# Two graph layers in one kernel: when the second layer's weights are loaded and combined, and the order of the last quad

## The chip, the cores and the metric

The kernel runs on one core of a Trainium2 chip. The metric is the device time of one execution in microseconds (us), lower is better. TensorE is called PE here, VectorE DVE, ScalarE ACT, GpSimd POOL and SyncE SP. SP computes nothing; it issues most of the DMA transfers, in order. POOL issues others between its computations.

## The reference

There are 128 graphs of 128 nodes with 512 features, all in fp32. In short:

```
h  = relu(layernorm(x))
# layer 0: attention over the graph, three hops
Xw = h @ Wv0 + bv;  sj = Xw @ aw[:512];  si = Xw @ aw[512:]
e  = leaky_relu(sj[:, None, :] + si[:, :, None] + ab, 0.2)
A  = adj * exp(e);  T = A / (sum(A, -1) + 1e-12)
x1 = x + relu(sum over k = 0, 1, 2 of (T^k h) @ Wk[k] + bk[k])
# layer 1
h2 = relu(layernorm(x1))
q, k = split(h2 @ Wqk);  v = h2 @ Wv1
w  = (512 ** -0.5) * mask * rowsum(q * (adj @ (k * mask)))
out = x1 + softmax(w over the nodes)[:, :, None] * v
```

The kernel folds q and k of layer 1 into one 512x512 matrix `M = Wq Wk^T`, so that w needs `h2 M` and `adj h2` alone. Layer 1 therefore multiplies h2 by one 512x1024 matrix, `rl`: its first half is M, its second `Wv1`.

## The kernel before

**Products.** Every large product is done with seven block products in place of eight (`strassen`, and `one_round` in layer 1): the blocks of the right matrix are combined by four subtractions (`combine`), those of the left by four more (`left_sums`, `inner_sums`), and the sums of the products are formed partly in the PSUM banks a, b, c and e. There are two sets of banks, `set1` (a1, b1, c1, e1) and `set2`. The chain inside a round is always the same: product 1 into a, ACT copies a to b; product 5 into e, ACT copies e to s; product 6 into b, ACT copies b to c; product 2 into a, which ends block (0, 0); product 7 into c, ACT copies c to s, and e + s ends block (1, 1); product 3 into b, b + s ends (0, 1); product 4 into c ends (1, 0).

**Layer 0** goes over 64 pairs of graphs (`for p in range(NP)`). PE multiplies by `r10` (`y10`, the hops 1 and 0), applies the transition matrix of the pair (`inner`, `outer`), and multiplies the pair after the next by `r2` (`y2`). Between these stand, on DVE, the block-wise transposes of h (`x<-hv`, L340) and their sums, the layer norm statistics, the attention, the transpose of the transition matrix (`tt<-junk`), and the sum that gives x1 (L616). A transpose takes a round trip through DRAM: h goes out (`hd<-h`, or `h2d<-h` for layer 1), comes back by blocks in four loads (`hv<-hd`, `hv<-h2d`), and DVE transposes 32x32 blocks. The transition matrix goes the same way (`td<-t`, `junk<-td`). For layer 1 the transposed h2 of a pair and its four sums are collected in `fw` (`for_layer1`, L407 to 441, one pair later) and stored as `fd` when a quad of graphs is complete, in two halves.

**The weights of layer 1.** `rl` is 512x1024. Its first half is computed in the setup, its second is loaded there (`rows(rl[:, :, 1], wv1)`). One outer combine (four subtractions of 128x1024) in pair 2 gives seven factors of 512x512 (`FACTORS`). In pairs 3 to 9 `prepare` combines one factor each (four subtractions of 128x256, into `stage`) and stores it to DRAM as `rwd`: one store of 512 KB and three of 128 KB. In pair 10 four of the seven factors are loaded as `rw`, the other three at the start of layer 1.

**Order.** A scheduler places the instructions of each engine; `behind(what, op)` tells it to issue an instruction only after the one recorded as `done[what]`. Since every engine and every DMA queue works in order, these marks fix who stands in front of whom. In layer 1 the order is written by hand: `put` (L651) chains each engine's instructions, and so do `dve`, `act`, `pool`, `sync` and `swdge`, as well as `ordered` for PE.

**Layer 1** goes over 32 quads (two pairs). Outer factors 1, 5, 2, 6 and then 3, 7, 4 are worked off in rounds, each of seven inner products of 128x256 a factor. `together` runs two rounds side by side, one step of each in turn; a dictionary of hooks says what other work follows each step. Outer results are added in `c`, a tile of four parts (`c[:, 0:4]`). Two of them, when complete, are `h2 M` of the two pairs and are multiplied with `agg = adj h2` for the scores (`scores`); the other two are the values. The scores of a quad lie in columns; to take the softmax over the nodes they are spread over rows, by a transpose and a round trip through DRAM (`spread_scores`, `pwd`, `pw`), and then DVE finds the peak (`peaks`), ACT takes exponentials (`exp_own`, `exp`), DVE the factor (`factors`), ACT scales the values (`scale`), POOL adds x1 by a DMA that accumulates (`add_x1`), and SP stores (`store`). All this runs one to two quads behind the products. The last quad (q = 31) has its own code: rounds (1, 6) and (2, 7) side by side, then 4, 5 and 3 by steps, and its two pairs of scores are spread by transposes on PE (`spread_pair`).

Of the kernel before, what the change touches and what calls it, by code (L numbers as in the profile page):

```python
# [16 lines left out]
def kernel(  # L17
# [32 lines left out]
    G = 2  # L50
# [136 lines left out]

    def combine(r, t):


        nc.vector.tensor_sub(t[0], r[0, 1], r[0, 0])
        nc.vector.tensor_sub(t[1], r[1, 1], t[0])
        nc.vector.tensor_sub(t[2], r[1, 1], r[0, 1])
        done["right"] = nc.vector.tensor_sub(t[3], r[1, 0], t[1]).ins
        return dict(zip((5, 6, 7, 4, 1, 2, 3), t + [r[0, 0], r[1, 0], r[1, 1]]))
# [81 lines left out]
    def statistics(src, gate="warm", middle=None):  # L277
# [13 lines left out]
        behind("aT" if middle else "warm", nc.vector.tensor_mul, r[:, 2], r[:, 1], r[:, 1])  # L291
# [34 lines left out]
    def by_blocks(h, hd=None):  # L326

        hd = dram.tile([G, P, D], FP, name="hd") if hd is None else hd
        nc.sync.dma_start(hd.rearrange("g n d -> n g d"), h)
        hv = front.tile([P, G, Q, P], FP, name="hv")  # L330
        v = hd.rearrange("g (q b) (c i) -> c b (g q) i", b=S32, i=P)
        for c in range(DC):
            at = hv[c * S32:(c + 1) * S32].rearrange("p g q i -> p (g q) i")
            done["hv"] = nc.sync.dma_start(at, v[c]).ins  # L334
        return hv
# [27 lines left out]
    def strassen(banks, left, right, s, first, ends, steps={}, gate="warm", seventh="warm"):  # L363
# [16 lines left out]
        done["ba"] = behind("warm" if first or "h2" not in done else "h2", nc.scalar.copy, b, a).ins  # L380
# [24 lines left out]
    SUMS = {}  # L405

    def for_layer1(p):  # L407
# [13 lines left out]
        if second:  # L421
# [3 lines left out]
            queue = nc.gpsimd if q + 1 < NQ else nc.sync  # L425

            def store_half(i):
                half = slice(4 * i, 4 * i + 4)
                queue.dma_start(fd[:, half].rearrange("p o n -> p (o n)"), fv[:, half].rearrange("p o n -> p (o n)"))  # L429

            def upper():
                behind("c12", nc.vector.tensor_sub, at[7], at[1], fv[:, L21])
                done["c12"] = nc.vector.tensor_sub(at[3], at[2], at[6]).ins
                store_half(1)
# [144 lines left out]
    def y10(p, steps):  # L579
# [6 lines left out]
        def end11(e, t):  # L586
# [8 lines left out]
            (1, 0): lambda c: None}, steps, "warm" if p else "z")  # L595
# [24 lines left out]
    def norm2(p):  # L620
# [6 lines left out]
        HV2[p] = by_blocks(h, H2D[p])  # L627
# [9 lines left out]

    def prepare(o, stage):
# [3 lines left out]
        combine(r, [t[:, i] for i in range(4)])  # L642
        behind("x1d", nc.sync.dma_start, RWD[o][:, :4], t)
        for i, at in enumerate(((0, 0), (1, 0), (1, 1))):
            behind("x1d", nc.sync.dma_start, RWD[o][:, 4 + i], r[at])
# [78 lines left out]
    with tc.issue_after(done["hv"]):  # L724
        load_x(3)
        load_adj(2)
        rows(rl[:, :, 1], wv1)
# [3 lines left out]
    for p in range(NP):  # L731
        def between():
# [6 lines left out]
            if p + 3 < NP:  # L739
                RS0[p + 3] = behind("left", statistics, xg[p + 3])  # L740
            if p == 2:
                rightl.update(behind("rs", combine, {(kh, k): rl[:, kh * HC:(kh + 1) * HC, k]
                                                     for kh in range(2) for k in range(2)},
                                     [tl[:, i] for i in range(4)]))
            if 3 <= p < 3 + len(FACTORS):
                behind("rs", prepare, FACTORS[p - 3], stage)
# [13 lines left out]
        if p > 0:  # L760
            behind("c12", for_layer1, p - 1)
        if p == NP - 2:
# [11 lines left out]
        behind("c12" if p else "left", outer, p, z)  # L774
        if p + 4 < NP:
            load_x(p + 4)
        if p == 0:
# [23 lines left out]
        if p == 3 + len(FACTORS):  # L801
# [3 lines left out]
            RW = {}  # L805
            for o in FACTORS[:4]:
                RW[o] = early.tile([P, 7, HD], FP, name=f"rw{o}")
                nc.sync.dma_start(RW[o], RWD[o])
# [34 lines left out]
    load_left(1, sync, (0,))  # L843
    load_left(1, swdge, (1,))
# [4 lines left out]
    def one_round(q, banks, factors, s, ends):  # L849
# [17 lines left out]
        def p5():  # L867
            product(e, 5, True)
            copy(s[:, 0], e)
# [9 lines left out]
        def p7():  # L879
            product(c, 7)  # L880
            copy(s[:, 1], c)
            ends[1, 1](v[3], sv[:, 1])

        def p3():
            product(b, 3)
            ends[0, 1](v[1], sv[:, 0])
# [111 lines left out]
    def catch_up(q):  # L998
# [4 lines left out]
        PW[q - 1] = spread_scores(W[q - 1])  # L1003
# [24 lines left out]
    for q in range(NQ - 1):  # L1028
# [28 lines left out]
        hooks = {0: sums[:2], 1: sums[2:]}  # L1057
        if q > 0:
# [23 lines left out]
    catch_up(q)  # L1082
    c, (s1, s2) = C[q], S.pop(q)
    x1 = back[2].tile([P, 2, G, D], FP, name="h2")
    for i in range(2):
        sync(x1[:, i], X1D[2 * q + i].rearrange("g n d -> n g d"))
    last_block(prior)
    soft = {}


    together(one_round(q, set1, (1, 6), s1, plain_ends(lambda i, j: c[:, 0:2, i, j])),
             one_round(q, set2, (2, 7), s2, adding_ends(
                 lambda i, j: c[:, 2:4, i, j],
                 lambda i, j: c[:, 0:1, i, j].to_broadcast([P, 2, HD]), True)),
             {2: lambda: scale(late, 1, 0), 3: lambda: scale(late, 1, 1)})
    add_x1(late, 1)

    dve(nc.vector.tensor_add, outer(q, 3), outer(q, 3), outer(q, 1))
    dve(nc.vector.tensor_add, outer(q, 1), outer(q, 0), outer(q, 1))
    soft[2] = peaks(W[prior], PW.pop(prior))  # L1100
    aggregate(q)
    for pair in range(2):
        store(late, pair)
    scores(q, 0, c[:, 2])


    r4 = one_round(q, set1, (4,), s1, adding_ends(lambda i, j: c[:, 0:1, i, j],
                                                  lambda i, j: c[:, 3:4, i, j], True))

    def sum_of_p5(end):  # L1110

        def both(*args, at):
            end(*args)
            for to in (1, 3):
# [103 lines left out]
```

## Time and profile before

| what | value |
|---|---|
| time, median of 3 runs | 2251.65 us (2249.95 to 2254.73) |
| the profiled execution's own time | 2251.06 us |
| its span, first to last instruction | 2249.3 us |
| PE busy | 2212.1 us, 98% |
| DVE, ACT, POOL busy | 74%, 55%, 31% |
| mean granted clock of PE | 0.996 |
| chain that ended last | PE 85%, DMA 6%, DVE 5% |
| DMA | 523.82 MB, 233 GB/s over the span |

Layer 0 lasts until about 1440 us, layer 1 from there to the end; the last quad starts at 2209. "Busy" counts from the first to the last element of an instruction. A granted clock of 1.00 is full speed, and 0.50 half of it.

### The profile page before, as it was taken

The page shows a single profiled execution, that of the slowest core. Times are in us where ns is not written, and L with a number is a line of the kernel's source. Part 1 is how long each engine was busy: PE and PEld are TensorE (multiplying, and loading weights), DVE is VectorE, ACT ScalarE, POOL GpSimd, SP SyncE. Part 2 cuts the span into 40 slices and gives each one's busy share as a digit, 9 for nine tenths or more (in the row PEclk, how much of TensorE's full clock was granted, in tenths as well). Part 3 has the DMA queues.
Part 4 walks back from the last instruction along what each step waited for, and adds up shares of the span by engine and source line. Part 5 has one row for each costly group of instructions (what it writes and reads, how often), then busy time and mean ns, then how long its engine had stood idle before and what let it go on. Part 6 is the DMA issues. An engine that isn't in the chain of part 4 may idle for free.

```text
span 2249.3 us, 29447 instructions
## 1 busy us (share of the span) xinstructions
PE 2212.1 (98%) x8109; PEld 1537.4 (68%) x8109; DVE 1666.1 (74%) x4524; ACT 1240.8 (55%) x2870; POOL 700.6 (31%) x828
## 2 busy tenths in 40 slices
PE   9999999999999999999999999999999999999997
PEld 5665656666566666666666666578888888888886
DVE  5777768777777777877778777577767767776777
ACT  3554545555554555545555555456666666666665
POOL 2121112121121211212112111145555555555554
PEclk9999999999999999999999999999999999999999
DMA  7688998777787887888778786767788888888887
GB/s 193 182 258 255 263 275 246 229 230 235 225 245 218 240 240 219 242 228 229 240 225 235 229 230 202 262 220 230 223 245 233 243 224 250 225 231 243 236 243 193
DMA packets 426467, 523.82 MB, mean 233 GB/s; under 512 B 100522, under 2 KB 281386, under 8 KB 409918
## 3 DMA queue, kind: packets, MB, share of 16 engines
q1 hardware_dynamic: 384876, 397.36, 58.7%
q0 software_dynamic: 41136, 124.04, 21.3%
q8 instruction: 65, 1.06, 0.2%
q14 instruction: 100, 0.82, 0.1%
q10 hardware_dynamic: 290, 0.53, 0.1%
HBM read 297.62 MB, written 224.18 MB: 232 GB/s over the span
## 4 chain that ended last, share of the span: by engine, by line
PE 85%; DMA 6%; DVE 5%; SPq 1%; ACT 1%; issue 1%; POOL 0%; DVEq 0%; ACTq 0%; POOLq 0%
PE a L91 25%; PE b L91 22%; PE c L91 22%; PE e L91 15%; DMA td<-t 1%; DMA hv<-h2d 1%; DMA hv<-hd 1%; SPq L334 1%; DMA tl<-in_L_gnn_Wqk_dram 1%; DMA pw<-pwd 1%; DMA atd<-aT 1%; DMA pwd<-pwt 1%; SPq L530 0%; DMA h2d<-h 0%; DVE fw L419 0%
## 5 line engine op out<-in xcount | busy, mean ns | idle before, releaser
L655 POOL TENSOR_TENSOR c<-s,c 128x512 f32<-128x512 f32 (+1 forms) x186 | 200.1, 1090 | 258.5 <-DVE s L655 253.7
L111 POOL DMA_DIRECT2D agb<-in_adj_dram x256 | 149.7, 591 | 340.9 <-DVE aT L86 248.2
L91 PE MATMUL a<-r,x 128*128 128x512 f32 x512 | 240.8, 592 | 0.2 <-issue 0.2
L91 PE MATMUL b<-rw,in 128*128 128x256 f32 x896 | 215.8, 381 | 0.1
L91 PEld LDWEIGHTS b<-rw,in 128*128 128x128 f32 x896 | 170.9, 191 | 23.9 <-ACT b L655 0.5
L429 POOL DMA_DIRECT2D fd<-fw x62 | 34.7, 559 | 477.4 <-DVE fw L437 283.6
L91 PEld LDWEIGHTS a<-r,x 128*128 128x128 f32 x512 | 97.1, 190 | 96.3 <-issue 92.9
L86 ACT COPY s<-c 128x257 f32<-128x257 f32 (+1 forms) x128 | 61.4, 479 | 174.6 <-PE c L91 174.5
L655 POOL TENSOR_TENSOR c<-c 128x1024 f32<-128x1024 f32 (+1 forms) x70 | 152.1, 2182 | 13.3 <-DVE c L655 13.0
L86 ACT COPY b<-a 128x257 f32<-128x257 f32 (+1 forms) x128 | 59.4, 464 | 165.8 <-PE a L91 165.8
L86 DVE TENSOR_TENSOR e<-e,s 128x512 f32<-128x512 f32 x64 | 44.7, 698 | 141.8 <-ACT s L86 141.8
L91 PE MATMUL a<-w,x 128*128 128x257 f32 x512 | 131.9, 380 | 1.2 <-DVE x L340 1.2
L91 PE MATMUL b<-w,sx 128*128 128x257 f32 x512 | 132.0, 380 | 0.0
L91 PE MATMUL b<-t,sx 128*128 128x512 f32 x256 | 120.6, 593 | 4.0 <-ACT b L86 4.0
L655 DVE SCALAR_TENSOR_TENSOR junk<-agg,wscale,c 128x512 f32<-128x512 f32 x128 | 98.7, 771 | 30.7 <-POOL c L655 25.8
L91 PE MATMUL c<-t,x 128*128 128x512 f32 x256 | 120.5, 593 | 0.2 <-ACT s L86 0.2
L91 PE MATMUL c<-t,sx 128*128 128x512 f32 x256 | 120.4, 593 | 0.0
L91 PE MATMUL e<-t,sx 128*128 128x512 f32 x256 | 120.3, 592 | 0.0
L91 PE MATMUL b<-r,sx 128*128 128x512 f32 x256 | 120.3, 592 | 0.0
L655 ACT ACTIVATE c<-c,wcol 128x512 f32<-128x512 f32 x125 | 87.1, 719 | 59.2 <-DVE wcol L655 58.3
L91 PE MATMUL c<-rw,in 128*128 128x256 f32 x448 | 109.0, 383 | 2.8 <-ACT c L655 2.7
L419 DVE STREAM_TRANSPOSE fw<-hv 128x256 f32<-128x256 f32 x256 | 90.9, 413 | 26.9 <-DMA hv<-h2d 26.8
(253 smaller groups left out, 5250.0 us busy)
## 6 DMA issues: line engine op xcount, KB each, us to landing
fd<-fw POOLq DMA_DIRECT2D x62, 1024.0 KB, 5.1
x1d<-x SPq DMA_DIRECT2D x64, 512.0 KB, 5.8
h2d<-h SPq DMA_DIRECT2D x64, 512.0 KB, 3.2
hv<-h2d SPq DMA_DIRECT2D x256, 128.0 KB, 4.2
xg<-in_x_dram SPq DMA_DIRECT2D x63, 512.0 KB, 6.1
hd<-h SPq DMA_DIRECT2D x63, 512.0 KB, 3.1
hv<-hd SPq DMA_DIRECT2D x252, 128.0 KB, 4.0
f<-fd SPq DMA_DIRECT2D x31, 1024.0 KB, 6.3
```

Source lines behind the costliest of these rows:

```text
L86: return op(*args, **how)
L91: done["mm"] = op(*args, **how).ins
L111: nc.gpsimd.dma_start(agb[p][c * S32:(c + 1) * S32].rearrange("p g q i -> p (g q) i"), v[c])
L334: done["hv"] = nc.sync.dma_start(at, v[c]).ins
L419: done["c12"] = nc.vector.transpose(blocks[:, k, j].rearrange("p f (n b) -> p f n b", n=Q), hv[:, j].rearrange("p n (k f a) -> p k f n a", ...
L429: queue.dma_start(fd[:, half].rearrange("p o n -> p (o n)"), fv[:, half].rearrange("p o n -> p (o n)"))
L655: done[engine] = op(*args, **how).ins
```

## The change

It has five parts.

1. Layer 1's weights are handled in single pieces over 19 pairs. Pairs 1 to 4 load one quarter of Wv1 each. Pairs 5 to 8 do one subtraction of the outer combine each, behind the transposes of `fw` and in front of x1. Pairs 9 to 15 prepare one factor each: two subtractions stand inside `statistics`, between ACT's logarithm and what DVE makes of it, the other two where the outer subtractions stood. Its four stores follow x1d on SP. Pairs 16 to 19 load one `rw` each.
2. In the last pair of layer 0 the copy b<-a no longer waits for the relu of h2 (`second`). The second half of `fd` 30 is stored by SP, between `h2d<-h` and `hv<-h2d` of the last pair, in place of POOL, and both halves of the left side of quad 1 are loaded by POOL.
3. In quad 0 the left sums for quad 1 follow steps 3 and 4 of the second group of rounds, no longer steps 0 and 1. In quad 1 the exponentials start one step later.
4. In the last quad, round (2, 7) lags round (1, 6). Banks are added where they lie with fewer copies (`direct`, `early`), further sums go to POOL (`u2`, `on_p5`). The scores of the quad before it are spread by four transposes on PE in place of the round trip through DRAM.
5. The rounds 4, 5 and 3 of the last quad change sets of banks and order; the scaled finish by ACT and POOL (`finish_scaled`) is dropped for a fourth `finish` on DVE.

The order of PE's instructions is the same up to the last quad.

```diff
+    def combine_steps(r, t):
+        def step(i, a, b):
+            done["right"] = nc.vector.tensor_sub(t[i], a, b).ins
+        return [partial(step, 0, r[0, 1], r[0, 0]), partial(step, 1, r[1, 1], t[0]),
+                partial(step, 2, r[1, 1], r[0, 1]), partial(step, 3, r[1, 0], t[1])]
+    def combined(r, t):
+        return dict(zip((5, 6, 7, 4, 1, 2, 3), t + [r[0, 0], r[1, 0], r[1, 1]]))
-        nc.vector.tensor_sub(t[0], r[0, 1], r[0, 0])
-        nc.vector.tensor_sub(t[1], r[1, 1], t[0])
-        nc.vector.tensor_sub(t[2], r[1, 1], r[0, 1])
-        done["right"] = nc.vector.tensor_sub(t[3], r[1, 0], t[1]).ins
-        return dict(zip((5, 6, 7, 4, 1, 2, 3), t + [r[0, 0], r[1, 0], r[1, 1]]))
+        for step in combine_steps(r, t):
+            step()
+        return combined(r, t)
...
-    def statistics(src, gate="warm", middle=None):
+    def statistics(src, gate="warm", middle=None, last="aT"):
...
-        behind("aT" if middle else "warm", nc.vector.tensor_mul, r[:, 2], r[:, 1], r[:, 1])
+        behind(last if middle else "warm", nc.vector.tensor_mul, r[:, 2], r[:, 1], r[:, 1])
...
-    def by_blocks(h, hd=None):
+    def by_blocks(h, hd=None, between=None):
+        if between:
+            between()
...
-    def strassen(banks, left, right, s, first, ends, steps={}, gate="warm", seventh="warm"):
+    def strassen(banks, left, right, s, first, ends, steps={}, gate="warm", second="warm", seventh="warm"):
...
-        done["ba"] = behind("warm" if first or "h2" not in done else "h2", nc.scalar.copy, b, a).ins
+        done["ba"] = behind(second, nc.scalar.copy, b, a).ins
...
-    SUMS = {}
+    SUMS, LAST = {}, []
...
-            queue = nc.gpsimd if q + 1 < NQ else nc.sync
+                queue = nc.gpsimd if q + 1 + i < NQ else nc.sync
-                store_half(1)
+                if q == NQ - 2:
+                    LAST.append(partial(store_half, 1))
+                else:
+                    store_half(1)
...
-            (1, 0): lambda c: None}, steps, "warm" if p else "z")
+            (1, 0): lambda c: None}, steps, "warm" if p else "z",
+            second="h2" if 0 < p < NP - 1 else "warm")
...
-        HV2[p] = by_blocks(h, H2D[p])
+        HV2[p] = by_blocks(h, H2D[p], LAST.pop() if p == NP - 1 else None)
...
+    FIRST = 1 + 2 * DC
+    OUTER = ({(kh, k): rl[:, kh * HC:(kh + 1) * HC, k] for kh in range(2) for k in range(2)}, [tl[:, i] for i in range(4)])
-        combine(r, [t[:, i] for i in range(4)])
-        behind("x1d", nc.sync.dma_start, RWD[o][:, :4], t)
-        for i, at in enumerate(((0, 0), (1, 0), (1, 1))):
-            behind("x1d", nc.sync.dma_start, RWD[o][:, 4 + i], r[at])
+        def store_all():
+            behind("x1d", nc.sync.dma_start, RWD[o][:, :4], t)
+            for i, at in enumerate(((0, 0), (1, 0), (1, 1))):
+                behind("x1d", nc.sync.dma_start, RWD[o][:, 4 + i], r[at])
+        return combine_steps(r, [t[:, i] for i in range(4)]), store_all
...
-        rows(rl[:, :, 1], wv1)
+        weights, weights_end = [], None
+        if DC < p <= 2 * DC:
+            weights = combine_steps(*OUTER)[p - DC - 1:p - DC]
+            weights_end = lambda: rightl.update(combined(*OUTER))
+        elif FIRST <= p < FIRST + len(FACTORS):
+            weights, weights_end = prepare(FACTORS[p - FIRST], stage)
...
-                RS0[p + 3] = behind("left", statistics, xg[p + 3])
-            if p == 2:
-                rightl.update(behind("rs", combine, {(kh, k): rl[:, kh * HC:(kh + 1) * HC, k]
-                                                     for kh in range(2) for k in range(2)},
-                                     [tl[:, i] for i in range(4)]))
-            if 3 <= p < 3 + len(FACTORS):
-                behind("rs", prepare, FACTORS[p - 3], stage)
+                two = weights[:2] if len(weights) > 2 else []
+                RS0[p + 3] = behind("left", statistics, xg[p + 3],
+                                    middle=(lambda: [behind("aggr", step) for step in two]) if two else None, last="right")
...
+        for step in weights[-2:]:
+            behind("c12", step)
+            done["c12"] = done["right"]
...
+        if weights:
+            weights_end()
+        if 0 < p <= DC:
+            behind("x1d", rows, rl[:, :, 1], wv1, (p - 1,))
...
-        if p == 3 + len(FACTORS):
+        if p == FIRST + len(FACTORS):
-            RW = {}
-            for o in FACTORS[:4]:
-                RW[o] = early.tile([P, 7, HD], FP, name=f"rw{o}")
-                nc.sync.dma_start(RW[o], RWD[o])
+            RW = {o: early.tile([P, 7, HD], FP, name=f"rw{o}") for o in FACTORS[:4]}
+        if FIRST + len(FACTORS) <= p < FIRST + len(FACTORS) + 4:
+            o = FACTORS[p - FIRST - len(FACTORS)]
+            behind("x1d", nc.sync.dma_start, RW[o], RWD[o])
...
-    load_left(1, sync, (0,))
-    load_left(1, swdge, (1,))
+    load_left(1, swdge)
-    def one_round(q, banks, factors, s, ends):
+    def one_round(q, banks, factors, s, ends, direct=False, early=None):
...
-            copy(s[:, 0], e)
+            if early:
+                early(v[3])
+            else:
+                copy(s[:, 0], e)
...
-            copy(s[:, 1], c)
-            ends[1, 1](v[3], sv[:, 1])
+            if early:
+                ends[1, 1](v[2])
+            elif direct:
+                ends[1, 1](v[2], sv[:, 0])
+            else:
+                copy(s[:, 1], c)
+                ends[1, 1](v[3], sv[:, 1])
-            ends[0, 1](v[1], sv[:, 0])
+            if early:
+                ends[0, 1](v[1])
+            else:
+                ends[0, 1](v[1], sv[:, 0])
...
-    def catch_up(q):
+    def catch_up(q, spread=True):
-        PW[q - 1] = spread_scores(W[q - 1])
+        if spread:
+            PW[q - 1] = spread_scores(W[q - 1])
...
-        hooks = {0: sums[:2], 1: sums[2:]}
-        if q > 0:
+        hooks = {3: sums[:2], 4: sums[2:]}
+        if q == 1:
+            hooks = {0: sums[:2],
+                     1: [lambda: exp_own(*soft), lambda: exp(*soft, 0)] + sums[2:],
+                     2: [lambda: exp(*soft, 1)],
+                     3: [lambda: exp(*soft, 2), lambda: exp(*soft, 3)],
+                     4: [lambda: factors(*soft)],
+                     5: [lambda: scale(prior, 0, 0)],
+                     6: [lambda: scale(prior, 0, 1)]}
+        elif q > 0:
...
-    catch_up(q)
...
+    catch_up(q, False)
+    c, (s1, s2) = C[q], S.pop(q)
...
+    def c_(k, i, j):
+        return c[:, k, i, j]
+    def in_place(to):
+        return lambda bank: dve(nc.vector.tensor_add, to, bank, to)
+    def u2(i, j):
+        pool(nc.gpsimd.tensor_add, c_(1, i, j), c_(0, i, j), c_(1, i, j))
+    def on_p5(i):
+        pool(nc.gpsimd.tensor_add, c[:, 2:4, i, 1], c[:, 0:2, i, 1], s2[:, 0].rearrange("p (k d) -> p k d", k=2))
+    def from_u2(i, j):
+        return lambda bank: dve(nc.vector.tensor_add, c[:, 2:4, i, j], bank, c[:, 0:2, i, j])
+    def on_top(i, j):
+        return lambda bank, t: in_place(c[:, 2:4, i, j])(bank)
+    ra = one_round(q, set1, (1, 6), s1, plain_ends(lambda i, j: c[:, 0:2, i, j]), direct=True)
+    rb = one_round(q, set2, (2, 7), s2, {(0, 0): from_u2(0, 0), (1, 1): on_top(1, 1), (0, 1): on_top(0, 1),
+                                         (1, 0): from_u2(1, 0)}, direct=True)
+    def a_h2(g):
+        pair, j = divmod(g, 2)
+        bank = (a1, b1, c1, e1)[g]
+        ordered(nc.tensor.matmul, bank, AT[q][:, pair, j], H2[q][:, pair, j], start=True, stop=True)
+        if pair:
+            copy(AGG[q][:, j], bank)
+    def spread_columns_of(w, bank, at, n):
+        spread = bank[:, :n * N] if n > G else bank[:, HD:]
+        spread = spread.rearrange("p (g n) -> p g n", g=n)
+        for j in range(n):
+            ordered(nc.tensor.transpose, spread[:, j], w[:, at + j:at + j + 1].to_broadcast([P, P]), ident)
+        return peaks(w, spread, at)
+    AGG[q] = back[0].tile([P, G, D], FP, name="agg")
+    def score(pair, j, y):
+        junk = back[0].tile([P, D], FP, name="junk")
+        b, at = (2 * q + pair) * G + j, pair * G + j
+        dve(nc.vector.scalar_tensor_tensor, junk, AGG[q][:, j] if pair else (a1, b1)[j], wscale[:, b:b + 1],
+            y[:, j].rearrange("p h d -> p (h d)"), op0=OP.mult, op1=OP.mult, accum_out=W[q][:, at:at + 1])
+    def steps(*order):
+        for round, i in order:
+            round[i]()
+    steps((ra, 0), (ra, 1), (ra, 2), (ra, 3))
+    u2(0, 0)
+    scale(late, 1, 0)
+    steps((rb, 0), (ra, 4))
+    u2(1, 1)
+    scale(late, 1, 1)
+    steps((ra, 5))
+    u2(0, 1)
+    soft[2] = spread_columns_of(W[prior], e1, 0, 2 * G)
+    steps((rb, 1))
+    exp_own(*soft[2])
+    exp(*soft[2], 0)
+    dve(nc.vector.tensor_add, outer(prior, 1), outer(prior, 3), outer(prior, 1))
+    steps((ra, 6))
+    u2(1, 0)
+    on_p5(1)
+    on_p5(0)
+    exp(*soft[2], 1)
+    exp(*soft[2], 2)
+    a_h2(0)
+    steps((rb, 2))
+    exp(*soft[2], 3)
+    factors(*soft[2])
...
+    scale(prior, 0, 0)
+    steps((rb, 3))
+    scale(prior, 0, 1)
+    a_h2(1)
+    a_h2(2)
+    scale(prior, 1, 0)
+    steps((rb, 4))
+    a_h2(3)
+    add_x1(prior, 0)
+    scale(prior, 1, 1)
+    add_x1(prior, 1)
+    steps((rb, 5))
+    score(0, 0, c[:, 2])
+    steps((rb, 6))
+    score(0, 1, c[:, 2])
...
+    for pair in range(2):
+        store(prior, pair)
+    r4 = one_round(q, set2, (4,), s2, {
+        (0, 0): lambda a: dve(nc.vector.tensor_add, c[:, 0:1, 0, 0], a, c[:, 3:4, 0, 0]),
+        (1, 1): in_place(c[:, 0:1, 1, 1]), (0, 1): in_place(c[:, 0:1, 0, 1]),
+        (1, 0): lambda a: dve(nc.vector.tensor_add, c[:, 0:1, 1, 0], a, c[:, 3:4, 1, 0])},
+        early=lambda e: dve(nc.vector.tensor_add, c[:, 0, :, 1], e.to_broadcast([P, G, HD]), c[:, 3, :, 1]))
+    def both(i, j):
+        to = c[:, 1::2, i, j]
+        return lambda bank, *t: dve(nc.vector.tensor_add, to, bank.to_broadcast([P, 2, HD]), to)
+    r5 = one_round(q, set1, (5,), s1, {at: both(*at) for at in ((0, 0), (1, 1), (0, 1), (1, 0))}, direct=True)
+    def p5_of_r5():
+        for k in (3, 1):
+            pool(nc.gpsimd.tensor_add, c[:, k, :, 1], c[:, k, :, 1], s1[:, 0:1, :HD].to_broadcast([P, G, HD]))
+    r3 = one_round(q, set2, (3,), s2, {at: in_place(c[:, 1:2, at[0], at[1]]) for at in ((0, 0), (1, 1), (0, 1), (1, 0))},
+                   early=lambda e: dve(nc.vector.tensor_add, c[:, 1, :, 1], e.to_broadcast([P, G, HD]), c[:, 1, :, 1]))
...
-    def finish_scaled(pair, j, v):
...
+    steps((r4, 0), (r4, 1), (r5, 0), (r5, 1))
+    p5_of_r5()
+    soft[0] = spread_columns_of(W[q], e1, 0, G)
+    steps((r4, 2), (r4, 3))
...
+    steps((r4, 4), (r5, 2), (r4, 5))
...
+    steps((r5, 3), (r4, 6))
+    score(1, 0, c[:, 0])
+    score(1, 1, c[:, 0])
+    steps((r5, 4), (r3, 0), (r5, 5), (r3, 1), (r5, 6), (r3, 2))
+    soft[1] = spread_columns_of(W[q], a1, G, G)
...
+    steps((r3, 3), (r3, 4), (r3, 5))
+    finish(0, 0, c[:, 1, 0], nc.scalar)
...
-    finish_scaled(1, 1, c[:, 3, 1])
...
+    finish(1, 1, c[:, 3, 1], nc.scalar)
+    finish(0, 1, c[:, 1, 1], nc.sync)
...
```

## The prediction

> **What bounds the kernel now.** I read the page first, then PE's waits and the busy times stretch by stretch, then the timeline where they point.
>
> ```profile
> span 2249.3 us, 29447 instructions
> PE 2212.1 (98%) x8109; PEld 1537.4 (68%) x8109; DVE 1666.1 (74%) x4524; ACT 1240.8 (55%) x2870; POOL 700.6 (31%) x828
> ...
> PE   9999999999999999999999999999999999999997
> ```
>
> PE is the bound, and it issues the same products after the change, with four transposes more. So only its 37 us without work, its clock and what follows its last product can move. The windows view shows where these are (the first number behind each stretch is its length, the second PE's busy time; clock, DMA share and GB/s come last):
>
> ```profile
> 150.00:420.00 270.00, 260.12 (x861) 161.99 (x860) 204.41 (x653) 137.64 (x325) 48.81 (x84) 1.00 0.88 255
> 420.00:700.00 280.00, 280.00 (x937) 177.52 (x936) 215.66 (x676) 148.27 (x351) 52.92 (x91) 1.00 0.79 232
> 1420.00:1500.00 80.00, 72.01 (x277) 52.72 (x276) 55.34 (x123) 36.21 (x78) 27.26 (x27) 0.98 0.66 243
> 2205.00:2250.00 45.00, 32.31 (x132) 25.02 (x130) 31.85 (x65) 22.96 (x62) 18.45 (x19) 0.91 0.69 173
> ```
>
> PE never stops from 420 to 1420, nor from 1500 to 2205. The three places with losses are the start of layer 0, the passage into layer 1 and the last quad: the three that the change touches. PE's waits in these windows, in that order (what waited, for what, us in total, times, longest):
>
> ```profile
> PE a L91 <- DVE tt L86: 7.1, 7, 2.0
> PE c L91 <- ACT s L86: 2.0, 3, 1.6
> ...
> PE b L91 <- ACT b L86: 2.9, 1, 2.9
> PE c L91 <- ACT c L655: 2.7, 1, 2.7
> PE e L91 <- DVE s L655: 1.7, 1, 1.7
> ...
> PE e L91 <- DVE c L655: 2.5, 1, 2.5
> ```
>
> **Part 1, the weights of layer 1.** In the timeline a pair's first product on `r10` follows that of the pair before by 21.54 us in pairs 13 to 61. Pairs 1 to 12 are longer by 15.2 us together: 1.9 in pairs 1 and 2, 7.3 in 3 to 9 (the prepare pairs), 6.0 in 10 to 12. One prepare pair, timeline:
>
> ```profile
> 248.22 0.42 DVE L616 SCALAR_TENSOR_TENSOR x<-a,xg 128x256 f32<-128x256 f32 x1
> 250.11 3.64 SPq L334 DMA_DIRECT2D hv<-hd  x4
> 259.22 1.30 DVE L340 STREAM_TRANSPOSE x<-hv 128x512 f32<-128x512 f32 x2 [3.20 <-DMA hv<-hd]
> 262.68 1.88 SPq L334 DMA_DIRECT2D hv<-h2d  x4
> 264.99 0.42 DVE L191 TENSOR_TENSOR stage<-tl 128x256 f32<-128x256 f32 x1
> 266.93 0.44 DVE L86 STREAM_TRANSPOSE tt<-junk 128x256 f32<-128x256 f32 x1
> 269.06 1.42 DVE L419 STREAM_TRANSPOSE fw<-hv 128x256 f32<-128x256 f32 x4
> 270.39 0.39 DVE L616 SCALAR_TENSOR_TENSOR x<-a,xg 128x256 f32<-128x256 f32 x1
> ```
>
> DVE's loop runs from one x1 (L616) to the next: the x1d store, h2d store and hv<-h2d loads on SP, the transposes of fw (call their start T), then x1 again. Here it takes 22.2 us. DVE stood 3.2 us because hv<-hd was queued behind x1d, and four subtractions (4 x 0.42) stood ahead of tt; that is the wait of PE for tt. The change leaves hv<-hd ahead of x1d, as in the later pairs, and puts two subtractions where DVE idles 0.6 us for ACT's logarithm (nearly free, and DVE is no longer late there). The other two, 0.84, stand between T and x1, in the loop. All four stores to rwd (0.92 MB) now stand on SP right behind x1d, ahead of xg, td, h2d and hv<-h2d. Their issue (0.34 to 0.64 each) fits in front of td, due 6.3 us behind x1; their transfer may not.
>
> The loop costs T, plus 1.42 for four transposes, plus on average 0.68 for the two sums of every second pair that stand before x1, plus what the change puts there. Where x1 is late and nothing disturbs it (pair 16: x1 at 15.6 into the pair), T is 18.3 behind x1: a loop of 20.4, under 21.54. Some 1.6 us of delay costs nothing (x1 at 14.4 in a steady pair, PE stopped from about 16.0 on).
> - Pairs 1 to 4: one load of 256 KB each. Zero to the 1.9 of before; I take 1.0.
> - Pairs 5 to 8: one 128x1024 subtraction, 1.25 (half of `c<-c` 128x1024 x2, 2.49, in the last quad). 18.3+1.42+0.68+1.25 = 21.65, or 0.1 each: 0.5. With T at 18.9: 2.8.
> - Pairs 9 to 15: what do 0.92 MB ahead of h2d cost? Two rows. A load of the same size (rw<-rwd in pair 10, behind h2d) left T at 18.72, 0.4 late. Two such loads ahead of pair 11's loads had T at 23.94, 5.6 late, 2.8 each. I take 1.2, nearer the single transfer: T 19.5. 19.5+1.42+0.68+0.84 = 22.44, 0.90 over, seven times 6.3, less 1.6: 4.7. The ends: T 18.3, a loop of 21.24, nothing; T 21.1, 2.5 over, 15.9.
> - Pairs 16 to 19: a load each at the place of pair 10's: T 18.72 fits. 0.5, at most 2.
>
> Sum 6.7 instead of 15.2: **8.5 gained**, between 15 gained and 7 lost.
>
> **Part 2, the passage** (PE at 1420 to 1500: 8.0 idle, and half clock from 1490.7 to 1494.1).
> - `second="warm"` puts the copy b<-a of the last pair ahead of the h2 relu. The 2.9 go; next late is t (DVE, 1428.15), about 0.6. Gain 2.3.
> - The second half of fd30 goes from POOL to SP, between hv<-h2d and x1d. POOL's rw loads no longer stand behind it, and the 0.6 for rw4 (landed 1456.60) goes. On SP it delays x1d by one issue, 0.5, with nobody waiting. Gain 0.6.
> - Sums of quad 0's hooks move from steps 0 and 1 to 3 and 4. DVE now meets the fw transposes earlier, and they wait for hv<-h2d of pair 63 (1463.27, after 1.58 idle). Behind them are queued a c<-a, the fw sums and s<-e, for which PE waits at e: 2.6 in place of 1.7. Loss 0.9.
> - Quad 1's exponentials move one step back, so that ACT copies s and c before it blocks on the peak (DVE's reduce waited 7.31 for pw<-pwd). The 2.7 go, and with them half clock for 3.4 us, 1.7 more. Gain 4.4.
>
> The clock behind the new 2.6: of the three gaps of 2.5 to 2.9 two were followed by 3.4 us at clock 0.50 (1490.7 and 2234.8), the one at 1424 by none. Two thirds of 1.7 would be 1.1; I take 0.9. The Trainium skill (TensorE: Matmul & The Clock Gate, What's actually happening) lets the clock fall only after an idle window of about 3.4 us; by it this wait costs nothing more and the part gains 6.4. The trace shows the fall after 2.5, so the trace decides.
>
> 2.3+0.6-0.9+4.4-0.9 = **5.5 gained**, between 2 and 8.
>
> **Part 3, the last quad.** Before, PE ends at 2240.40 and DVE's last finish at 2245.89, 3.4 ahead of the span's end. Laid end to end by the rows (two passes 0.43, two transposes 0.22, a bank's sum 0.36, ACT copies 0.35 and 0.56, POOL 128x512 1.25), the new order loses 4.0 on PE in several places, the longest 1.7 at c1, which DVE has not read; before it was 2.5 in one place and 1.7 by the clock at 0.50. Four transposes cost 0.44. PE ends near 2238.7: 1.7 earlier. Behind PE's end DVE had 0.43+1.84+0.41+0.43+0.75+0.42+0.75, with short gaps 5.5. Now it has a recip and product, a sum and three finishes (0.75), partly ahead of PE's end: 3.8. The 1.84 is a finish stretched by POOL's sum beside it (2241.38, 1.26), which goes. **3.4 gained**; 5.5 if no copy of a bank is late, nothing if DVE is the bound of the whole last third.
>
> Against this stands that the scores of pair 1 now run beside POOL's sums of product 5. Such an operation took 2.94 instead of 0.75 at 1453.47, with POOL adding. The Trainium skill says the same (GPSIMD Engine Reference, Specifications): its SBUF interface is shared with VectorE, with contention at two SBUF inputs. By the rule for both scores, with the 1.09 of the 1.84, the part gains only 1.2. I leave 3.4, since the finishes behind them wait for product 3 anyway.
>
> **Sum.** 8.5+5.5+3.4 = 17.4. The profiled execution took 2251.06 (span 2249.3 and 1.8 around it), 0.6 under the median 2251.65 that I compare with: 2234.3, rounded **2234**. A measurement can tell 0.2%, 4.5 us, from no change.
>
> **Rivals.**
> - *The stores to rwd hold every prepare pair (slower).* Seen in pair 11: h2d issued 11.4 behind x1 instead of 7.3, T at 23.94. The loop is then 26.88, 5.3 over, seven times 37.4 less 1.6, and 2 for the rest: 37.8 against 15.2, 22.6 lost, 8.9 gained elsewhere: 2265. It decides over 0.2% once these pairs exceed 21.54 by 4.0, T above 22.6. Against it: half of pair 11's transfers. For it: DMA is at 0.88 in this window. Chance 0.08.
> - *The stores cost nothing* (T 18.3): layer 0 loses 2, 13.2+5.5+3.4 = 22.1 gained, 2229.5. Chance 0.17.
> - *The passage keeps its loss*: DVE's earlier wait for hv<-h2d takes back what the copies give. 2239.8. Chance 0.12.
> - *The last third is DVE's*: no gain in part 3. 2237.7. Chance 0.13.
> - The forecast: 0.50.
>
> The forecast alone reaches from 2229.5 to 2245.5 (T 18.3 to 21.1, the other parts at their values); with the ends of the other parts (a passage that gains only 2, or 8; no gain at the end) 2226 to 2250 leaves out 2 in 10. Above 2247.1, within 0.2%, lies the upper end of part 1 with a weak passage: same 0.13, slower 0.10, faster 0.77.
>
> **What would show it.** Right: no wait for tt in 150 to 420, some 5 us of waits in pairs 9 to 15 and next to none in 16 to 19; T near 19.5; the waits 2.9 and 2.7 gone, one of 2.6 at e near 1466; PE's end near 2238.7 less the gains before it, the last store 3.8 plus 3.4 behind it. Wrong: T beyond 21 in the prepare pairs, a stop over 3 us in the passage, or half clock again in the last quad.

## The result and the profile after

The changed kernel takes 2237.64 us (median of 4 runs, 2235.75 to 2238.32) against 2250.8 us before (4 runs, 2246.99 to 2254.73). The ratio is 0.994, with a 95% interval from 0.9921 to 0.9959: faster by some 13 us. The prediction was 2234, within 2226 to 2250, and faster with 0.77. The profiled execution took 2236.97 us, its span 2235.2. The page after:

```profile
span 2235.2 us, 29424 instructions
...
PE 2207.0 (99%) x8113; PEld 1536.1 (69%) x8113; DVE 1658.9 (74%) x4521; ACT 1235.8 (55%) x2858; POOL 698.5 (31%) x825
```

PE is busy for 5.1 us less, though it has four instructions more: it ran for less time at half clock (mean granted clock 0.998, before 0.996). Some 3.4 of the 5.1 us belong to 6.8 us at half clock in the setup of before, which are chance, as the first experiment shows. Its waits in the start of layer 0 (150 to 460), in the passage (1410 to 1490) and in the last quad (2185 to 2240):

```profile
PE c L91 <- ACT s L86: 8.0, 7, 1.5
...
PE e L91 <- DVE s L674: 3.1, 1, 3.1
PE b L91 <- ACT b L674: 0.9, 1, 0.9
PE a L91 <- DVE c L674: 0.7, 1, 0.7
...
PE c L91 <- DVE c L674: 1.7, 2, 1.2
PE e L91 <- ACT s L674: 1.0, 1, 1.0
PE b L91 <- ACT b L674: 0.8, 1, 0.8
```

The waits for tt, 7.1 us before, are gone here; a second profile of the changed kernel has two of them, 2.0 together. Seven waits of about 1.1 at c for s have come, one in each of pairs 10 to 16. In the passage 2.9 and 2.7 are gone, and the 1.7 at e has become 3.1. In the last quad the single 2.5 has become several smaller ones.

Where the time went is read best by cutting the span at five marks of PE: the first product on `r10` of pair 0 and of pair 63, the first product of the aggregation of quad 2 and of quad 30, and the end. The table was worked out from the timelines of the profiled executions. Both kernels were profiled twice:

| us | to pair 0 | pair 0 to 63 | to quad 2 (passage) | to quad 30 | to the end |
|---|---|---|---|---|---|
| before | 43.26 | 1377.37 | 87.91 | 688.38 | 52.36 |
| before again | 38.41 | 1381.71 | 92.09 | 688.38 | 51.96 |
| after | 40.87 | 1372.24 | 84.48 | 688.38 | 49.23 |
| after again | 40.20 | 1379.67 | 85.05 | 688.38 | 50.00 |

The quads in between are the same to 0.01 us. The setup varies by itself, and so does the start of layer 0, by several us: a single profile settles no difference of 3 us in those columns.

### The profile page after: what moved, and what is told of

Same layout as the page of the kernel before. It is cut to its first block, busy times and chain, and to the rows that moved or that the text cites. A ratio compares the mean times of both kernels' runs of the same rounds, so it can differ in the third digit from the quotient of the medians.

```text
span 2235.2 us, 29424 instructions
## 1 busy us (share of the span) xinstructions
PE 2207.0 (99%) x8113; PEld 1536.1 (69%) x8113; DVE 1658.9 (74%) x4521; ACT 1235.8 (55%) x2858; POOL 698.5 (31%) x825
## 4 chain that ended last, share of the span: by engine, by line
PE 87%; DVE 5%; DMA 5%; SPq 2%; issue 1%; ACT 1%; DVEq 0%; POOL 0%; ACTq 0%
PE a L91 25%; PE b L91 23%; PE c L91 23%; PE e L91 15%; DMA td<-t 2%; DMA hv<-h2d 1%; SPq L542 1%; DMA tl<-in_L_gnn_Wqk_dram 1%; DVE fw L429 1%; SPq L344 0%; DMA h2d<-h 0%; DVE c L674 0%; SPq L86 0%; DVE x L629 0%; DVE st L290 0%
## 5 line engine op out<-in xcount | busy, mean ns | idle before, releaser
L674 POOL TENSOR_TENSOR c<-c 128x1024 f32<-128x1024 f32 (+1 forms) x65 | 146.2, 2249 | 15.7 <-DVE c L674 13.4
L91 PE MATMUL e<-rw,in 128*128 128x256 f32 x448 | 109.1, 383 | 3.1 <-DVE s L674 3.1
```

The costliest lines, as they stand in the source:

```text
L91: done["mm"] = op(*args, **how).ins
L674: done[engine] = op(*args, **how).ins
```

## The experiments

**The setup.** In the two first profiles the change seemed to gain 2.4 us before pair 0 began. The kernel before was profiled again.

> The kernel before once more, with a profile of its own. The first product on r10 came at 43.26 in the profile of before and between 38.1 and 40.9 in five profiles of kernels with the change. Theory (half clock in the setup falls by chance, so that these 2.4 us are not the change's): it comes anywhere between 38 and 43.3 here. Rival (the load of Wv1 in the setup costs it): it comes at 43 again.

Pair 0 began at 38.41, as early as in kernels with the change. By the granted clock the first profile of before had half clock from 16.1 to 23.0 us, under the products that give M, and this one has full clock from 11.0 on. The 2.4 us are chance, and a part of the spread of the times. The waits for tt are there again (150 to 420):

```profile
PE a L91 <- DVE tt L86: 7.7, 7, 2.0
PE c L91 <- ACT s L86: 2.2, 5, 0.7
PE b L91 <- ACT b L86: 1.4, 1, 1.4
```

**Prepare pairs: the subtractions.**

```diff
-                two = weights[:2] if len(weights) > 2 else []
+                two = weights if len(weights) > 2 else []
...
-        for step in weights[-2:]:
+        for step in weights if len(weights) == 1 else []:
```

> All four subtractions of a prepared factor stand in the statistics; none is left between the fw transposes and x1. Theory (in pairs 10 to 16 the loop from x1 to x1 is the bound: T, set by the landing of hv<-h2d behind the stores, plus 1.42, 0.68 and 0.84): the loop loses its 0.84, so PE's waits at c for s in pairs 10 to 16 fall from 8.0 us to about 8.0 - 7 x 0.84 = 2.1, with T unchanged at 19.5 to 21.2 behind x1. Rival (DVE itself is the bound, so that two subtractions cost the same wherever they stand): the waits stay near 8.

The waits at c fell from 8.0 to 4.2, where six profiles of kernels with the change unaltered there have 6.8 to 9.5, and two waits for tt, 0.8 together, came. So taking two subtractions out of the loop gave 3.8 of the 5.9 us expected at c, and 3.0 with the waits for tt counted. Whether the subtractions delay T where they now stand isn't shown: T (from x1 to the transposes of fw) was 20.4 to 21.4 in pairs 13 to 15, against 19.4 to 21.2 in the first profile of the changed kernel and 20.3 to 20.9 in its second, which also has waits for tt. Pair 0 to 63 took 1371.94, inside the spread of the six (1371.09 to 1379.67). Both theories are half right, and the time itself tells nothing.

**Prepare pairs: the place of the stores.**

```diff
-            behind("x1d", nc.sync.dma_start, RWD[o][:, :4], t)
+            behind("hv", nc.sync.dma_start, RWD[o][:, :4], t)
...
-                behind("x1d", nc.sync.dma_start, RWD[o][:, 4 + i], r[at])
+                behind("hv", nc.sync.dma_start, RWD[o][:, 4 + i], r[at])
...
-        if weights:
-            weights_end()
...
         norm2(p)
+        if weights:
+            weights_end()
```

> The four stores to rwd stand on SP behind hv<-h2d in place of behind x1d. Theory (0.92 MB ahead of h2d make hv<-h2d land late, at 19 to 21 behind x1): the loads land at 17 to 18.5 as in the later pairs, T falls to 18.3 to 19, and the waits at c for s fall from 8.0 us to under 2. Rival (the bytes have to pass within the pair anyway): the delay moves to hd and hv<-hd, and PE waits for tt or for s, 6 us or more in all.

Pair 12 after the change, chosen lines of the timeline:

```profile
329.12 0.41 DVE L629 SCALAR_TENSOR_TENSOR x<-a,xg 128x256 f32<-128x256 f32 x1
330.97 1.25 SPq L86 DMA_DIRECT2D rwd<-stage  x1
332.27 3.30 SPq L86 DMA_DIRECT2D rwd<-tl  x3
336.73 1.37 SPq L337 DMA_DIRECT2D h2d<-h  x1
343.94 1.88 SPq L344 DMA_DIRECT2D hv<-h2d  x4
350.29 1.42 DVE L429 STREAM_TRANSPOSE fw<-hv 128x256 f32<-128x256 f32 x4 [2.50 <-DMA hv<-h2d]
352.27 0.42 DVE L629 SCALAR_TENSOR_TENSOR x<-a,xg 128x256 f32<-128x256 f32 x1
```

The same pair with the stores behind the loads, chosen lines:

```profile
323.00 0.42 DVE L629 SCALAR_TENSOR_TENSOR x<-a,xg 128x256 f32<-128x256 f32 x1
336.52 1.87 SPq L344 DMA_DIRECT2D hv<-h2d  x4
338.43 0.45 SPq L86 DMA_DIRECT2D rwd<-stage  x1
338.93 1.92 SPq L86 DMA_DIRECT2D rwd<-tl  x3
342.20 1.42 DVE L429 STREAM_TRANSPOSE fw<-hv 128x256 f32<-128x256 f32 x4 [1.04 <-DMA hv<-h2d]
344.19 0.41 DVE L629 SCALAR_TENSOR_TENSOR x<-a,xg 128x256 f32<-128x256 f32 x1
```

The loop falls from 23.15 to 21.19 us, T from 21.2 to 19.2. DVE's idle time before the transposes, put down to hv<-h2d, falls from 2.50 to 1.04. Over pairs 9 to 15 T is 18.7 to 19.7, a little above the 18.3 to 19 expected. The waits at c fell from 8.0 to 1.2 in this profile, and pair 0 to 63 took 1366.01 against 1372.24. The price that the rival named is small: in pairs 11, 13, 15 and 16 hv<-hd now comes behind x1d (DVE waits 0.8 to 3.4 us for it, 2.2 in pair 13), and PE has no wait for tt at all. The same edit, timed:

> The stores to rwd behind hv<-h2d, timed. Theory (they held T): 7 to 8 us under the changed kernel, 2229 to 2231, with pairs 1 to 16 in 348 to 350. Rival (one lucky profile): within 3 us of it.

2233.8 us (median of 5) against 2239.68 for the changed kernel on the same chip: 5.9 us, a little less than the 7 to 8 expected, and the two sets of runs don't overlap (2230.45 to 2236.11, and 2236.48 to 2245.10). In this profile the waits at c were 3.6 in place of the 1.2 of the first, pairs 1 to 16 took 352.6 and not 348 to 350, and pair 0 to 63 took 1370.96.

**Prepare pairs: fewer bytes at a time.** Each factor is spread over two pairs (9 to 22), with two subtractions in the statistics and some half of the stores in each (0.39 MB in the odd pairs, 0.52 in the even ones), still behind x1d.

```diff
+            i = (p - FIRST) % 2
+            if i == 0:
+                factor = prepare(FACTORS[(p - FIRST) // 2], stage)
+            weights, weights_end = factor[0][2 * i:2 * i + 2], partial(factor[1], i)
```

> Each factor is prepared over two pairs (9 to 22): two subtractions, both in the statistics, and half of the stores (0.46 MB) per pair, still behind x1d; the loads of rw follow in pairs 23 to 26. Theory (T is set by the bytes ahead of h2d, 2.1 later than the 18.3 of an undisturbed pair for 0.92 MB): half of that, T near 19.4; with no subtraction in the loop 19.4+2.1 = 21.5, so PE's waits at c for s fall from 8.0 us to under 1.5 in all. Rival (a store costs by its place or its number, not its bytes): T stays above 20 and 14 pairs lose 0.5 or more each, 7 us or more.

The waits at c in 150 to 460 are 1.5, one for tt of 0.7 follows, and pair 0 to 63 took 1367.22: about as good as the other place. But T wasn't near 19.4 throughout: it was 18.4 to 21.7, 19.8 on average, above 20 in pairs 9, 10, 12, 16, 19, 20 and 22. In the changed kernel, with equal bytes in each pair, T alternates already: 20.8, 21.2 and 21.2 in pairs 10, 12 and 14, 19.5, 19.4 and 19.6 in pairs 11, 13 and 15. With fewer bytes the odd ones fell to 18.5, 18.4 and 19.4, but the even ones were 21.7, 21.0 and 19.6, hardly earlier. The theory was right in the sum and wrong on T. How much a store in front delays hv<-h2d is not a simple price per byte here.

**The passage: the order of the sums.**

```diff
-        hooks = {3: sums[:2], 4: sums[2:]}
+        hooks = {0: sums[:2], 1: sums[2:]}
```

> In quad 0 the left sums for quad 1 follow steps 0 and 1 again, as before the change; all else is as after it. Theory (DVE waits 3.2 us for hv<-h2d of pair 63 and then has two of these sums in front of s<-e, for which PE waits 3.1): the two sums, 1.3, are done before the wait; PE waits 1.7 to 1.9 at e, and half clock behind it goes or stays by its luck: quad 0 to quad 1 takes 28.6 to 30.3 in place of 31.5. Rival (the loads of f land at 1447.8 and DVE stands before them instead): PE waits at a for c<-a, and quad 0 to 1 stays at 31 or more.

The outcome is the rival's, but not its cause. The wait at e is gone, and in its place is a single one, twice as long:

```profile
PE a L91 <- DVE c L674: 6.1, 1, 6.1
PE a L91 <- DVE t L529: 0.2, 1, 0.2
```

The timeline shows what DVE stands for:

```profile
1443.21 0.69 DVE L674 TENSOR_TENSOR in<-f 128x512 f32<-128x512 f32 x1
1450.18 1.42 DVE L429 STREAM_TRANSPOSE fw<-hv 128x256 f32<-128x256 f32 x4 [6.28 <-DMA hv<-h2d]
1455.71 1.21 DVE L674 TENSOR_TENSOR c<-a,c 128x512 f32<-128x512 f32 x2
```

It isn't f that DVE waits for: the two halves of f had landed 13.1 and 15.7 us after their issue at 1429.6 and 1430.1, by 1445.8. After the first sum DVE stands 6.3 us in front of the transposes until hv<-h2d has landed, with the other sums and c<-a behind them. The clock was at half for 6.8 us, from 2.7 us before the end of PE's wait. Quad 0 to quad 1 took 33.0 us, which is inside the 30.8 to 34.4 of the eight profiles with steps 3 and 4 and the wait of 3.1 (their waits there are 3.9 to 5.8 in all, and their half clock lasts from 3.4 to 10.2). So undoing steps 3 and 4 doesn't undo the cost; that they are the better place is likely by PE's waits, but one profile doesn't show it in the time.

**The passage: what holds h2d.** After the change, pair 63 goes as follows (chosen lines of the timeline):

```profile
1433.45 1.05 POOL L674 DMA_DIRECT2D f<-fd  x2
1438.97 0.37 SPq L337 DMA_DIRECT2D h2d<-h  x1
1449.18 1.94 SPq L344 DMA_DIRECT2D hv<-h2d  x4
1453.93 1.42 DVE L429 STREAM_TRANSPOSE fw<-hv 128x256 f32<-128x256 f32 x4 [3.22 <-DMA hv<-h2d]
1459.19 1.01 DVE L674 TENSOR_TENSOR s<-e,s 128x512 f32<-128x512 f32 x2
```

SP waits 10.2 us for a store of 512 KB (9.8 in the same place before the change). The DMA engines are full from 1431 to 1448, from 1435 on with rw and then with f; the store's first packets move at 1442 and then go out among f's. Two edits: the second half of f behind hv<-h2d of pair 63, and both halves.

```diff
-    load_left(1, swdge)
+    load_left(1, swdge, (0,))
+    with tc.issue_after(done["hv"]):
+        load_left(1, sync, (1,))
```

> The second half of the left side of quad 1 (1 MB) is loaded by SP behind hv<-h2d of pair 63, no longer by POOL ahead of h2d<-h. Theory (the store h2d<-h of pair 63 takes 10 us because 4.8 MB of POOL's loads are ahead of it): it lands about 4 us earlier, near 1445, hv<-h2d near 1450, DVE's wait of 3.2 falls to nothing, PE's 3.1 at e to under 1 without half clock; quad 0 to 1 takes 27 to 28 in place of 31.5. Rival (the 2.7 MB of rw set that time): the store lands as late, and nothing changes.

```diff
-    load_left(1, swdge)
+    with tc.issue_after(done["hv"]):
+        load_left(1, sync)
```

> Both halves of the left side of quad 1 are loaded by SP behind hv<-h2d of pair 63, none by POOL ahead of h2d<-h. Theory (the packets of h2d<-h go out one by one between the 8 KB packets of f, and a DMA engine that lags with these ends the store): the store lands near 1443 to 1445, hv<-h2d at 1447 to 1449, DVE's wait of 3.2 is under 1, PE's 3.1 at e is gone, without half clock; quad 0 to quad 1 takes 26 to 28 in place of 31.5. Rival (f is then late itself): PE waits at a or e for f or its sums, 2 us or more, and quad 0 to 1 stays above 30.

With one half little moved: the loads of hv were issued 9.8 us behind h2d<-h in place of 10.2, the 3.1 stayed, and quad 0 to 1 took 30.8, with half clock for 3.4 us. Most of the store's packets were out by 1446, but it landed at 1448.4: its last packets and those of f kept trickling until then (DMA was at 0.08 and 0.06 from 1446 to 1448). Why is open. The rival's outcome came, but its reason covers the start alone: the store's packets began to move at 1442, when those of rw were nearly out, and rw had landed by 1444.9. With both halves behind, the loads of hv are issued 6.1 us behind h2d<-h in place of 10.2, DVE doesn't wait for them, and the wait at e falls to 0.9:

```profile
PE b L91 <- ACT b L674: 2.4, 1, 2.4
PE e L91 <- DVE s L674: 0.9, 1, 0.9
```

But quad 0 to 1 takes 30.1, not 26 to 28. DVE works without a pause from the transposes at 1449.20 to the end of s<-b at 1459.4, and ACT's b<-a waits for that s<-b: what is late next is DVE's own queue. A part of its length is two sums that take longer beside POOL's:

```profile
1453.36 0.69 DVE L674 TENSOR_TENSOR in<-f 128x512 f32<-128x512 f32 x1
...
1455.52 2.40 POOL L674 TENSOR_TENSOR c<-s,c 128x512 f32<-128x512 f32 x2 [11.21 <-DVE s L674]
1455.62 1.72 DVE L674 TENSOR_TENSOR in<-f 128x512 f32<-128x512 f32 x1
1457.26 1.21 DVE L674 TENSOR_TENSOR in<-f,in 128x512 f32<-128x512 f32 x1
1458.39 1.01 DVE L674 TENSOR_TENSOR s<-b,s 128x512 f32<-128x512 f32 x2
1459.16 1.06 ACT L674 COPY b<-a 128x512 f32<-128x512 f32 x2 [8.46 <-DVE s L674]
```

At 0.69 each the two would end some 1.5 us earlier, most of the 2.4 at b; that is an estimate from these rows and was not tried. Half clock for 3.4 us stayed too, from 1459.8 on.

**The end: is it DVE?** Left out is one DVE sum of 0.68 in the last round, so that part of the values lacks product 5.

```diff
-                   early=lambda e: dve(nc.vector.tensor_add, c[:, 1, :, 1], e.to_broadcast([P, G, HD]), c[:, 1, :, 1]))
+                   early=lambda e: None)
```

> The sum of product 5 of the last round (factor 3) onto c, one DVE operation of 128x512 (0.68), is left out; the values of the second halves are then short of it. Theory (from 2222 on DVE has no gap and sets PE's 1.2 at c and the end): DVE's last finish and the end come 0.6 to 0.7 earlier behind the start of the last quad. Rival (PE's own products set the end): less than 0.2.

From the aggregation of the last quad to DVE's last finish it takes 24.16 us instead of 24.44 after the change (24.44 or 24.45 in all ten profiles with this part unaltered): 0.3 of the 0.68. One of the two waits at c for DVE went (0.5), the other of 1.2 stayed. DVE holds the end, but not alone.

**Both edits that helped.**

> The changed kernel once more, with a profile of its own, beside the next two. Theory: 2235 to 2239, 13 us under before; its first pairs up to 17 take 384 to 388 from the first product on r10, its passage from pair 63 to the aggregation of quad 2 84 to 87, by the half clock in it. Rival (the gain in its first profile was largely chance): under 9 us over these rounds.

> Both: the stores to rwd behind hv<-h2d, and the left side of quad 1 loaded behind hv<-h2d of pair 63. Theory (separate places, so the gains add): 1 to 3 us under the one before, near 2228; the stop at e under 1, one of 2.4 at b for ACT's copy b<-a, which waits for DVE. Rival (DVE's queue in the passage takes as long either way): the same time as the one before, within 1 us.

| us, same chip | median | runs | ratio to before, 95% |
|---|---|---|---|
| before | 2251.41 | 9 | 1 |
| changed kernel | 2239.68 | 5 | 0.9954 (0.9941 to 0.9967) |
| stores behind hv<-h2d | 2233.8 | 5 | 0.9923 (0.991 to 0.9935) |
| and f behind hv<-h2d of pair 63 | 2228.85 | 4 | 0.99 (0.9885 to 0.9916) |

The changed kernel gained 11.7 us here, a little less than the 13 expected; its pairs 0 to 16 took 391.0 in this profile and not 384 to 388. The last row beats both kernels: 22.6 us under the kernel before. The second step, 5.0 between the medians, is more than was expected, but its runs (2227.76 to 2236.00) overlap with those of the row above, so that its size is loosely known. In the profiles the passage gains 3.4 (83.15 in the last against 86.56 in the one before it), and these two executions took 2236.00 and 2236.11 in all; the rest wasn't taken apart.

## Why the prediction was right, and where its terms were off

The time lies in the range and the direction holds in all three places, but the sum, 17.4, was too large by 4 to 6, and two of the three signs that the prediction itself gave for being wrong appeared: T beyond 21 in three of the seven prepare pairs, and a stop over 3 us in the passage. The terms for the copy b<-a and the exponentials hold. Those for the stores, for quad 0 to 1 and for the two halves of the last quad don't. No run has one part of the change by itself: how the gain divides among the places is read from the marks and from the waits that went.

*Start of layer 0: 8.5 predicted, about 5 measured.* Six profiles of kernels with the change unaltered in this part took 1371.1 to 1379.7 from pair 0 to 63, 1374.3 on average; the two of before 1377.4 and 1381.7. The waits for tt went, as predicted, or nearly (2.0 in the second profile). Which of the two reasons did it isn't shown: hv<-hd ahead of x1d, or two subtractions fewer ahead of tt. Where the stores' place put hv<-hd behind x1d again, with DVE standing up to 3.4 us, PE waited for tt by 0.4 at most, so hv<-hd alone isn't the reason. Two terms were mis-sized:
- The stores. T was taken at 19.5. It was 20.4 on average in pairs 9 to 15 (21.2, 20.8, 19.5, 21.2, 19.4, 21.2, 19.6), and pairs 10 to 16 run over by 1.4 each, 9.8 together, not 4.7. The row chosen for the price, a load of the same size in pair 10, stood *behind* h2d; the stores stand ahead of it. Their issue alone held SP for 4.6 us in pair 12 (0.82 to 1.25 each), where 0.34 to 0.64 each was allowed; the 0.64 is a mean over merged rows, and single ones took up to 1.00 before. Even so h2d was issued no later, 7.6 us behind x1 in pair 12 and 7.5 before; what is late is its landing. The 9.8 lie halfway between the 4.7 and pair 11's bound, 15.9. The experiment with the stores' place shows that it is this place that makes T late: behind hv<-h2d T is 19.2 on average in these pairs, and 19.4 in the second profile.
- Pair 0 was left out of the sum. It took 30.76 and 31.87 before and 29.51 after: without Wv1's megabyte in pair 0 DVE's wait for hv<-hd (1.2 and 2.2 us of PE) is gone. That it is this load was not tried by itself. That this gain made up for a part of the stores' cost is luck.

In the first profile pairs 5 to 8 lose nothing (0.5 taken), pairs 1 to 4 lose 1.6 (1.0 taken), and pairs 17 to 19 lose nothing.

*The passage: 5.5 predicted, 3.4 in the two first profiles, about 4 over more* (86.0 on average in seven profiles with this part unaltered, 87.9 and 92.1 before). Pair 63 up to quad 0's aggregation gained 2.6 (2.3 for the copy b<-a), and quad 1 to 2 4.5 (4.4 for the exponentials): both to 0.3. The failed term is quad 0 to 1, for which -0.9 for the hook, -0.9 for the clock and +0.6 for rw4 were taken, -1.2. It went from 27.79 to 31.47, -3.7, and that was the mildest of the seven profiles: they took up to 34.4, 33.0 on average. In the first it was 3.1 in place of 2.6 at e, 0.7 more at a ahead of it and 0.9 at b behind it, and the whole of the half clock. What the term lacked is the rest of DVE's queue. It priced the wait for s<-e alone; the c<-a ahead of it, which it names, has PE wait too, and so has s<-b behind it, for which ACT's b<-a and then PE wait. With the loads of hv brought forward until DVE no longer waited for them, 2.4 at b were left, so the queue itself, with the sums that take longer beside POOL's, is too long in this place.

*The last quad: 3.4 predicted, 3.1* (2.8 on average over all profiles). The sum holds, the halves don't, and that their errors cancel is luck. PE's end gained 0.4 and not 1.7. That 1.7 doesn't follow from the prediction's own figures: 2.5 and 1.7 before against 4.0 and 0.44 after make a loss of 0.2. Behind PE's end 2.8 were gained and not 1.7: DVE's last finish came 3.1 behind it in place of 5.5, where 3.8 was taken, and the last store 3.0 behind that in place of 3.4. The tail behind PE is now

```profile
2228.69 0.75 DVE L674 SCALAR_TENSOR_TENSOR h<-c,wcol,h 128x512 f32<-128x512 f32 x1
...
2229.75 0.75 DVE L674 SCALAR_TENSOR_TENSOR h<-c,wcol,h 128x512 f32<-128x512 f32 x1
2230.42 0.42 DVE L674 TENSOR_TENSOR c<-c,c 128x256 f32<-128x256 f32 x1
2230.75 1.41 DVE L674 SCALAR_TENSOR_TENSOR h<-c,wcol,h 128x512 f32<-128x512 f32 x2
```

with no finish stretched to 1.84. The fear for the scores beside POOL was idle: POOL's sums of product 5 were done at 2221.1 and the scores began at 2223.0, at 0.75 each. The rule on the shared interface was not put to the test there. At quad 0's score it shows as before: 2.94 us at 1443.35, with POOL's 128x1024 sum from 1443.39.

*The clock.* The Trainium skill (TensorE: Matmul & The Clock Gate, What's actually happening) lets the clock fall after an idle window of about 3.4 us. Here eight profiles have the same wait of 3.1 in the passage, with waits of 0.4 to 1.2 ahead of it in seven, and half clock set in between 2.1 us ahead of its end and 5.0 behind it: for 3.4 us in four, 6.8 in one and 10.2 in three. The stop of 2.9 at 1424, which had no half clock in the first profile of before, had 3.4 us of it in the second. The trace decides: near such a wait the price must be taken whole, up to three times 1.7, and no two thirds of it.

## What to carry to other kernels

A transfer is priced by what it stands in front of: the same 0.9 MB cost 0.2 to 0.4 us a pair behind the round trip that the loop waits for, and 1.4 ahead of it. When a wait moves forward in an engine's queue, follow the queue behind it until it has caught up, and price every wait on the way, not the first alone. Before a difference of a few us is explained from two profiles, profile the same kernel twice.

## What the runs showed of the hardware that was not expected

- Taking 1 MB of the 4.8 ahead of a store away need not bring it forward. With one half of f ahead of it in place of two the store of 512 KB still took 9.8 us from issue, the last two with DMA nearly idle; with none of f, 6.1 and 6.4 in two profiles.
- SP's issue of a store to rwd, 0.34 to 1.00 us in the profile of before, took 0.82 to 1.25 in pair 12 after the change, where DMA was full, and that of h2d<-h behind them 1.37.
- Half clock in the setup came and went from profile to profile of the same kernel, with 4.9 us between the two starts of pair 0. In the passage stops of 0.9 and 2.4 us, 2.0 apart, were enough for 3.4 us of it (both halves of f behind hv<-h2d).
- A DVE sum of 128x512 that takes 0.69 by itself took 1.72 beside two POOL sums of the same size, and the next one 1.21.
